# A decoder layer on one core: the shared expert's first 1024 tokens by seven half-size products, with their sums made in earlier stages

## The chip, the core and the metric

The kernel runs on one core of a Trainium2 chip. The metric is device time in microseconds for one execution. TensorE (PE) multiplies, with weight loads (PEld) beside it; VectorE (DVE), ScalarE (ACT) and GpSimd (POOL) do the elementwise work; SyncE (SP) issues nearly all transfers, one after the other, each holding up the ones behind it while it waits for a tile to come free.

## What is computed

4096 tokens of 512 numbers pass through three residual blocks, all in 32-bit floats: a first attention against fixed keys and values with a squared ReLU, a cross attention to 128 context tokens with 16 heads, and a mixture of experts. Each block works on a layer norm of its input. The block that the change touches is the last, cut to what matters:

```python
x = hidden_states.reshape(-1, h)                       # 4096 x 512, the normalised tokens ("z" in the kernel)
shared_out = _swiglu(x, shared_gate_w, shared_up_w, shared_down_w)   # every token; 512 -> 1024 -> 512
logits = x @ gate_w                                    # 32 experts, the best one per token
topk_ids = jnp.argmax(logits, axis=-1)
topk_val = jnp.max(logits, axis=-1)
xs = x * jax.nn.sigmoid(topk_val)[:, None]
# ... tokens sorted by expert, routed_out = the chosen expert's swiglu of xs ...
return shared_out + routed_out                         # added to the residual
# _swiglu(x, gw, uw, dw) = (silu(x @ gw) * (x @ uw)) @ dw
```

## The kernel before

Every 32-bit factor of a matmul is split into a high part (rounded by ACT, `split`, L94) and a low part (the difference, L97, by DVE or POOL), and each product is three matmuls: low by high, high by low, high by high (`three`). A product costs so the matmuls and, once for each factor, two elementwise operations.

Stages follow each other on the tokens. Instructions are recorded in the order in which Python emits them; a scheduler then sets the order on each engine from priorities (`later` lowers one) and from its own estimate of when inputs are ready. Background work is given as generators, and `next(...)` at chosen places sets how far it goes.

- **Stage 0** (`stage0`, about 0 to 785 us): the first attention, 8 tiles of 512 tokens, 4 heads, 16 key blocks each. A score step is three matmuls into a bank of P1 or P2, a ReLU on ACT (L349), the square on DVE (L353), a split, and, seven steps later, three value matmuls (L309). Its background is `context_steps`: keys, values and weights of the cross attention. From the second tile on one background step is taken at `kt % 8 == 6` in every head but the first.
- **Stage 1** (`stage1`, to about 1440 us): the cross attention, 16 tiles of 256 tokens, four groups `q4` of four heads each: `queries`, `scores`, `turn`, `values`, `outputs` at distances of up to five groups. `finish(t)` adds the residual (`xr`, written to `x2`), normalises, transposes (`tr`), splits and stores z (`zT`), stores the unsplit z (`zF`, for tiles past the third), and makes the router's logits (`lt`, `lg`). Its background, near the end, is `shared_weights`.
- **Shared expert** (`shared`, about 1387 to 1830 us): hidden columns 0 to 767, in three pairs of 128-column blocks; the last 256 columns are spread over the routed stage. For tokens 1024 to 4095, three groups G of 1024, each pair p takes Strassen-Winograd's form: a 2 x 2 block product by seven half-size products (`PRODUCTS`, in the order `TURN`), with sums of z (S1 to S4) and of weights (T1 to T4). For the first 1024 tokens the product is plain: `plain_up` (L926, banks P3 and P2) and `plain_down` (L940), in two halves of 512 tokens.
- **Routed experts** (`routed`, to the end).

`Pairs.sums(p)` loads the four weight blocks of a pair (`in_sgu`), forms the four sums (L853), splits them and stores both parts in DRAM (`wS`); `Pairs.steps(p, w)` gives the seven weight tiles of a pair, four split from the raw blocks and three read back from `wS`. Before, `sums(0)` and `sums(1)` run beside the plain products and `sums(2)` in the first step of G = 1. `sums(g, zF, G, ...)` loads z from `zF` and makes S1 to S4, which `load_z` then splits.

In a (G, p) step, `up` makes 7 products x 2 (gate, up) x 2 x 3 matmuls of 512 columns (L975), `down` of the step before follows in `between`; `acc` gathers the pairs and the residual.

Large tiles come from few pools: A to K in one, `raw` (6 tiles) for what is loaded and then split, `W` (45 tiles) for weights, and PSUM banks P1 to P4, two of each.

Of the kernel before, what the change touches and what calls it, by code (L numbers as in the profile page):

```python
# [22 lines left out]
C = 512  # L23
# [15 lines left out]
PAIRS = 3  # L39
# [130 lines left out]
def context_steps(g, ctxT, wk, wv, wq, wo, kst, vst):  # L170
# [28 lines left out]
    for c in range(2):  # L199
        v = yield from weight_steps(g, wv[:, c * 512:(c + 1) * 512], 4, 512, "wv", pool)  # L200
        for b in range(2):
# [12 lines left out]
            yield  # L214
    g.wq2 = yield from weight_steps(g, wq, 4, 1024, "wq", pool)
# [4 lines left out]
def stage0(g, x, wfcT, wpT, lnT, x1, background):  # L220
# [107 lines left out]
    for i, (t, h, kt) in enumerate(steps):  # L328
# [6 lines left out]
        if t > 0 and h > 0 and kt % 8 == 6:  # L335
            with g.after(*marks):
                next(background, None)
# [34 lines left out]
def stage1(g, x1, mask, kst, vst, gate, x2, zT, zF, xs, ef, background):  # L372
# [146 lines left out]
    def finish(t):  # L519
# [3 lines left out]
        for s in range(2):  # L523
            v = g.tile("G", "xr")
            nc.sync.dma_start(v[:], x1[rows[s], :])
            z.append(v)
# [62 lines left out]
    for _ in range(2):  # L589
        go(pre, 1, prep)  # L590
    queries(0, 0)
    queries(0, 1)
    for i in range(4 * NT + 12):
# [22 lines left out]
        for _ in range({4 * NT - 2: 5, 4 * NT + 2: 3}.get(i, 0)):  # L616
            next(background)
# [163 lines left out]
def shared_weights(g, wg, wu, wd):  # L781

    g.sw = {}
    for name, w in (("g", wg), ("u", wu)):
        g.sw[name] = o = [[], []]
        for k in range(4):
            if k % 2 == 0:
                pair = [g.piece("sw", (128, 2, 256)) for _ in range(2)]
            for z in range(2):
                o[z].append([g.piece("sw")[:], pair[z][:, k % 2, :]])  # L790
            yield from split_steps(g, w[k * 128:k * 128 + 128, 0:768], o[0][k:], o[1][k:])
    g.sw["d"] = yield from weight_steps(g, wd[0:768, :], 6, 512, "sd")

# [107 lines left out]
def load_z(g, zT, SUM, G, name, engine):  # L901

    z = z_tiles(g, name)
    for j in range(2):
        if name[0] == "S":
# [8 lines left out]
def shared(g, zT, zF, x2, out, pairs, wd, routing, rest, rest_weights):  # L914
    nc = g.nc
    NG = T // 1024
    Z, H, ACC, SUM = {}, {}, {}, {}

    def plain_up(t, c, z):
        o = []  # L920
        for nm, tag in (("g", "P3"), ("u", "P2")):
            p = g.bank(tag, nm)
            n = 0
            for k in range(4):
                for w, y in three((g.sw[nm], z)):
                    nc.tensor.matmul(p[:], part(w, k, c), y[k][:], start=n == 0, stop=n == 11)  # L926
                    n += 1
            o.append(p)
        s = g.tile("H", "s")
        nc.scalar.activation(s[:], o[0][:], AF.Silu)  # L930
        nc.vector.tensor_tensor(o[1][:], o[1][:], s[:], A.mult)
        hh, hl = g.tile("C", "hh", FR), g.tile("D", "hl", FR)
        split(g, hh[:], hl[:], o[1][:])
        H[t, c] = (hh, hl)

    def plain_down(t, s):
        o = g.bank("P1" if t == 0 and s > 1 else "P4", "d")
        for c in range(2 * PAIRS):
            for n, (w, y) in enumerate(three((g.sw["d"], H[t, c]))):
                nc.tensor.matmul(o[:], y[:, s * 128:(s + 1) * 128], w[c][0], start=c == 0 and n == 0, stop=c == 2 * PAIRS - 1 and n == 2)  # L940
        b = g.tile("I", "b")
        nc.sync.dma_start(b[:], x2[rows(0, t, s), :])
        nc.vector.tensor_tensor(b[:], o[:], b[:], A.add)
        nc.sync.dma_start(out[rows(0, t, s), :], b[:])
# [72 lines left out]
    w = {}  # L1017
    parts = sums(g, zF, 1, SUM, nc.vector)
    ahead = chain(pairs.sums(0), pairs.sums(1), pairs.steps(0, w))
    for t in range(2):  # L1020
        z = [[g.tile(("EF", "AB")[t][i], f"z{i}", FR) for _ in range(4)] for i in range(2)]
        for k in range(4):
            for i in range(2):
                nc.sync.dma_start(f32(z[i][k][:]), zT[i, :, k, t * 512:(t + 1) * 512])
        for c in range(2 * PAIRS):
            if c == 1 and t > 0:
                for s in range(4):
                    plain_down(0, s)
            plain_up(t, c, z)
            if t == 1 or c > 1:  # L1030
                next(ahead, None)
                if t == 1 and c < 3:
                    next(ahead, None)
            if t == 1:
                next(parts, None)
    for n in TURN:
        a = PRODUCTS[n][1]
        Z[a] = load_z(g, zT, SUM, 1, a, nc.vector)
        next(ahead, None)
    run(ahead)  # L1040
    pairs.engine = nc.gpsimd
    steps = [(G, p) for G in range(1, NG) for p in range(PAIRS)]
    before, parts = [lambda s=s: plain_down(1, s) for s in range(4)], None
    for n, (G, p) in enumerate(steps):
# [6 lines left out]
        more = pairs.sums(2) if n == 0 else None  # L1051

        def between(a):
# [5 lines left out]
            if p == PAIRS - 1 and G + 1 < NG:  # L1059
                Z[a] = load_z(g, zT, SUM, G + 1, a, nc.gpsimd)  # L1060
            if before:
                before.pop(0)()
            if more:
                next(more, None)
# [495 lines left out]
```

## Time and profile before

| | us |
|---|---|
| median of 3 runs | 2699.37 (2699.36 to 2700.18) |
| the profiled execution | 2698.85 |
| its span, first to last instruction | 2697.1 |
| PE busy | 2639.6 |
| DVE busy | 2033.8 |
| ACT busy | 1873.8 |
| POOL busy | 1129.3 |

The profile is of one execution. Its windows give each engine's busy time in a stretch of the span and, after an "x", how many instructions touch it; PEclk is the share of full clock that TensorE was granted. Matmuls overlap: the duration of one is longer than the distance between two starts. A row of instructions reads: line, engine, operation, output from inputs, count, shortest, median and longest duration in ns.

### The profile page before, as it was taken

What the parts mean: (1) busy time and instruction counts of PE and PEld (TensorE: products, weight loads), DVE (VectorE), ACT (ScalarE), POOL (GpSimd) and SP (SyncE); (2) the same over time, 40 slices, a digit from 0 to 9 for tenths busy, and PEclk for the clock granted to TensorE, in tenths of its full rate; (3) what the DMA queues carried; (4) which work ended last, traced back from release to release, by engine and by line L of the source; (5) the groups of instructions that cost most, each with busy time, mean ns of one, the idle gap of its engine ahead of it and who ended that gap; (6) DMA issues with size and microseconds to landing.
All of it is one profiled execution on the core that took longest, in us unless ns stands there. A gap on an engine that the chain in (4) does not pass through costs nothing. (4 is left out here: it accounts for less than half of the span.)

```text
span 2697.1 us, 47526 instructions
## 1 busy us (share of the span) xinstructions
PE 2639.6 (98%) x14629; PEld 2274.4 (84%) x14629; DVE 2033.8 (75%) x4559; ACT 1873.8 (69%) x4152; POOL 1129.3 (42%) x911
## 2 busy tenths in 40 slices
PE   7999999999999999999999999999999999999998
PEld 5878888887879999999987878778889898888886
DVE  7777777777777888888876596564776777778995
ACT  7788787888778877877874333333666777767885
POOL 5576566666654334444440547620122122212321
PEclk9999999999999999999999999999999999999999
DMA  4112112212020224232249846673899899999994
GB/s 154 32 63 87 55 67 81 77 43 83 30 86 27 87 76 138 96 108 90 102 158 327 273 140 239 223 214 109 260 287 276 279 302 292 299 280 291 325 324 142
DMA packets 269409, 446.68 MB, mean 166 GB/s; under 512 B 33536, under 2 KB 77568, under 8 KB 269152
## 3 DMA queue, kind: packets, MB, share of 16 engines
q1 hardware_dynamic: 254464, 416.46, 45.6%
q0 software_dynamic: 14688, 27.17, 5.1%
q8 instruction: 116, 1.90, 0.3%
q14 instruction: 141, 1.16, 0.1%
HBM read 348.83 MB, written 96.64 MB: 165 GB/s over the span
## 5 line engine op out<-in xcount | busy, mean ns | idle before, releaser
L97 DVE TENSOR_TENSOR rl<-raw,rh 128x512 fp32r<-128x512 f32 x768 | 488.2, 683 | 90.6 <-ACT rh L94 64.0
L94 ACT CAST rh<-raw 128x512 fp32r<-128x512 f32 x768 | 438.3, 621 | 141.6 <-DMA raw<-in_rg 98.2
L97 POOL TENSOR_TENSOR pl<-p,ph 128x512 fp32r<-128x512 f32 x320 | 411.4, 1297 | 264.3 <-ACT ph L94 210.0
L349 ACT ACTIVATE rl<-s 128x512 f32<-128x512 f32 x512 | 293.2, 604 | 38.2 <-PE s L345 30.6
L1336 POOL DMA_INDIRECT out_dram<-v,idx x46 | 114.2, 2483 | 463.6 <-ACT v L1334 368.7
L470 POOL TENSOR_TENSOR e<-e,ri 128x512 f32<-128x512 f32 x128 | 132.8, 1043 | 305.8 <-DVE ri L468 159.4
L353 DVE TENSOR_TENSOR p<-s,rl 128x512 f32<-128x512 f32 x320 | 215.1, 683 | 41.7 <-ACT rl L349 39.1
L94 ACT CAST ph<-p 128x512 fp32r<-128x512 f32 x320 | 199.2, 626 | 60.1 <-DVE p L353 57.4
L467 ACT ACTIVATE e<-e,mn 128x128 f32<-128x128 f32 x512 | 199.9, 392 | 27.9 <-DVE mn L462 26.7
L345 PE MATMUL s<-qh,kwl 128*128 128x512 f32 x512 | 205.5, 403 | 6.4 <-DVE p L353 3.1
L309 PE MATMUL o<-pl,vwh 128*128 128x512 f32 x512 | 203.1, 397 | 2.2 <-POOL pl L97 2.2
L353 DVE TENSOR_TENSOR s<-s,rl 128x512 f32<-128x512 f32 x192 | 133.3, 694 | 91.2 <-ACT rl L349 90.8
L309 PE MATMUL o<-ph,vwl 128*128 128x512 f32 x512 | 200.9, 394 | 1.0 <-ACT ph L94 1.0
L345 PE MATMUL s<-ql,kwh 128*128 128x512 f32 x512 | 200.3, 391 | 0.0
L345 PE MATMUL s<-qh,kwh 128*128 128x512 f32 x512 | 200.1, 391 | 0.0
L309 PE MATMUL o<-ph,vwh 128*128 128x512 f32 x512 | 199.6, 390 | 0.0
L975 PE MATMUL gu<-z,swh 128*128 128x512 f32 x504 | 158.3, 392 | 0.0
L440 PE MATMUL q<-yh,wql 128*128 128x256 f32 x512 | 147.3, 288 | 1.5 <-ACT yh L94 0.6
L97 DVE TENSOR_TENSOR pl<-s,ph 128x512 fp32r<-128x512 f32 x192 | 131.1, 683 | 21.1 <-ACT ph L94 18.6
L440 PE MATMUL q<-yh,wqh 128*128 128x256 f32 x512 | 146.3, 286 | 0.0
L440 PE MATMUL q<-yl,wqh 128*128 128x256 f32 x512 | 145.9, 285 | 0.0
L345 PEld LDWEIGHTS s<-qh,kwl 128*128 128x128 f32 x512 | 96.6, 189 | 33.1 <-DVE p L353 8.6
(361 smaller groups left out, 7958.0 us busy)
## 6 DMA issues: line engine op xcount, KB each, us to landing
raw<-in_rg SPq DMA_DIRECT2D x256, 256.0 KB, 5.4
raw<-in_ru SPq DMA_DIRECT2D x256, 256.0 KB, 5.4
raw<-in_rd SPq DMA_DIRECT2D x256, 256.0 KB, 5.3
z<-zT SPq DMA_DIRECT2D x116, 256.0 KB, 5.6
b<-x SPq DMA_DIRECT2D x40, 256.0 KB, 3.0
raw<-in_sgu SPq DMA_DIRECT2D x39, 256.0 KB, 4.2
swh<-wS SPq DMA_DIRECT2D x36, 256.0 KB, 4.9
swl<-wS SPq DMA_DIRECT2D x36, 256.0 KB, 4.9
```

The lines of the kernel that those rows point to most:

```text
L94: g.nc.scalar.copy(hi, src)
L97: g.low = (lo_engine or g.nc.vector).tensor_tensor(lo, src, f32(hi), A.subtract)
L309: nc.tensor.matmul(o[:], w, y[:], start=kt == 0 and n == 0, stop=kt == 15 and n == 2)
L345: nc.tensor.matmul(s[:], w, y[:], start=n == 0, stop=n == 2)
L349: m0 = nc.scalar.activation(r[:], s[:], AF.Relu)
L353: m1 = nc.vector.tensor_tensor(p[:], s[:], r[:], A.mult)
L440: nc.tensor.matmul(o[:, i, :], part(w, k, p), y[k // 2][:, k % 2, :], start=n == 0, stop=n == 11)
L467: nc.scalar.activation(e[:, hs], e[:, hs], AF.Exp, bias=mn[:, h:h + 1], scale=-1.0, accum_out=su[:, h:h + 1])
L470: nc.gpsimd.tensor_tensor(e4, e4, ri[:].unsqueeze(2).to_broadcast([128, 4, 128]), A.mult)
L975: nc.tensor.matmul(o[:], y, z, start=(at, x) not in begun, stop=j == 1 and m == 2, skip_group_check=True)
L1336: nc.gpsimd.indirect_dma_start(out=out, out_offset=bass.IndirectOffsetOnAxis(ap=idx[rows, b + j:b + j + 1], axis=0), in_=v[rows], in_offse ...
```

## The change

The first 1024 tokens become the group G = 0 of the same seven-product path, so the plain path and its weights (`shared_weights`) go, and the steps are twelve instead of nine.

- `Pairs.sums(0)` to `sums(2)` move into stage 0, into `context_steps`, two sums to a step, with the low parts on DVE. To make room, background steps are also taken in the heads 2 and 3 of the first tile.
- `zF` is stored for all tiles. `first_sums`, called once in every second group from group 28 to group 59 of stage 1, forms S1 to S4 of the first 1024 tokens from it, splits them and stores them in a new DRAM tensor `zS`.
- `first_steps` replaces `shared_weights` as stage 1's background: weight tiles and inputs of the first step (G = 0, p = 0), of which S inputs are read from `zS`.
- The residual tile `xr` of the last two tiles of stage 1 comes from `raw` rather than G; `up` takes its banks in the order P3, P2, P1 rather than P1, P2, P3.
- Routing (`route`) advances from the third step of twelve rather than from the first of nine.

```diff
 # context_steps, between the values' weights and wq
+    for p in range(PAIRS):
+        steps = g.pairs.sums(p)
+        for _ in steps:
+            next(steps)
             yield
 ...
 # stage0
-        if t > 0 and h > 0 and kt % 8 == 6:
+        if (h > 0 if t > 0 else h > 1) and kt % 8 == 6:
             with g.after(*marks):
                 next(background, None)
 ...
+def first_sums(g, zF, zS):
+
+    V = g.nc.vector
+    for j in range(2):
+        for q in range(2):
+            cols = slice(q * 256, q * 256 + 256)
+            a = []
+            for half, tag in enumerate("rC"):
+                shape = [128, 2, 256]
+                v = g.raw.tile(shape, F32, name="sa", tag="raw") if tag == "r" else g.tile(tag, "sb", F32, shape)
+                at = half * 512 + q * 256
+                g.nc.sync.dma_start(v[:], zF[:, :, at:at + 256].rearrange("p (c j) n -> p j c n", j=2)[:, j, :, :])
+                a.append(v)
+            yield
+            (p, r), s = a, g.W.tile([128, 2, 256], F32, name="sc", tag="W")
+            V.tensor_tensor(s[:, 0, :], r[:, 0, :], r[:, 1, :], A.add)
+            V.tensor_tensor(r[:, 0, :], p[:, 0, :], r[:, 0, :], A.subtract)
+            V.tensor_tensor(s[:, 1, :], s[:, 0, :], p[:, 0, :], A.subtract)
+            V.tensor_tensor(r[:, 1, :], p[:, 1, :], s[:, 1, :], A.subtract)
+            yield
+            for n, v in ((0, s), (2, r)):
+                hi, lo = g.tile("C", "sh", FR, (128, 2, 256)), g.tile("D", "sl", FR, (128, 2, 256))
+                split(g, hi[:], lo[:], v[:])
+                for i, x in enumerate((hi, lo)):
+                    g.nc.sync.dma_start(zS[i, n:n + 2, :, j, cols].rearrange("n p c -> p n c"), f32(x[:]))
+                yield
 ...
 # finish
-            v = g.tile("G", "xr")
+            v = g.tile("G", "xr") if t < NT - 2 else g.raw.tile([128, 512], F32, name="xr", tag="raw")
 ...
-            for c in range(2 if t > 3 else 0):
+            for c in range(2):
                 v = g.tile("D", "zf", F32, (128, 2, 256))
 ...
 # stage1's loop over groups
-        for _ in range({4 * NT - 2: 5, 4 * NT + 2: 3}.get(i, 0)):
-            next(background)
+        if 28 <= i < 60 and i % 2:
+            next(early, None)
+        if i > 4 * NT - 3:
+            next(background, None)
+        if i in (4 * NT - 2, 4 * NT - 1, 4 * NT):
+            next(background, None)
 ...
 # load_z
+        if name[0] == "S" and G == 0:
+            for i in range(2):
+                g.nc.sync.dma_start(f32(z[j][i][:]), zS[i, int(name[1]) - 1, :, j, :])
+            continue
 ...
+def first_steps(g, zT, zS, w, Z):
+
+    ahead = g.pairs.steps(0, w)
+    for n in TURN:
+        a = PRODUCTS[n][1]
+        if a in ("A11", "S2", "S1"):
+            Z[a] = load_z(g, zT, zS, None, 0, a, None)
+        next(ahead)
+        yield
+    for n in TURN:
+        a = PRODUCTS[n][1]
+        if a not in Z:
+            Z[a] = load_z(g, zT, zS, None, 0, a, None)
+            yield
 ...
 # up
-        banks = [[g.bank(tag, "gu") for _ in range(2)] for tag in ("P1", "P2", "P3")]
+        banks = [[g.bank(tag, "gu") for _ in range(2)] for tag in ("P3", "P2", "P1")]
 ...
 # shared: plain_up, plain_down, shared_weights and the loop over the two plain halves go
-    ahead = chain(pairs.sums(0), pairs.sums(1), pairs.steps(0, w))
 ...
-    steps = [(G, p) for G in range(1, NG) for p in range(PAIRS)]
-    before, parts = [lambda s=s: plain_down(1, s) for s in range(4)], None
+    steps = [(G, p) for G in range(NG) for p in range(PAIRS)]
+    before, parts = [], None
 ...
-        more = pairs.sums(2) if n == 0 else None
 ...
-            next(routing, None)
+            if n > 1:
+                next(routing, None)
```

More of the change, by code (lines that the diff above doesn't have):

```diff
@@ L369, in place, with stage1 @@
     return slice(at * 256, at * 256 + 256)
-def stage1(g, x1, mask, kst, vst, gate, x2, zT, zF, xs, ef, background):
+def first_sums(g, zF, zS):
[23 more added lines that the diff above has]
+                yield
+def stage1(g, x1, mask, kst, vst, gate, x2, zT, zF, zS, xs, ef, background):
     nc = g.nc
@@ L590, in stage1 @@
         go(pre, 1, prep)
+    early = first_sums(g, zF, zS)
     queries(0, 0)
@@ L777, in route @@
     nc.sync.dma_start(ids[:], parts[0][:])
[L781 to L792, printed above, removed]
 PRODUCTS = {1: (0, "A11", "B11"), 2: (0, "A12", "B21"), 3: (2, "S4", "B22"), 4: (1, "A22", "T4"),
@@ L898, in z_tiles, with load_z @@
     return [[g.tile(next(tags), "z", FR) for _ in range(2)] for _ in range(2)]
-def load_z(g, zT, SUM, G, name, engine):
+def load_z(g, zT, zS, SUM, G, name, engine):
     z = z_tiles(g, name)
     for j in range(2):
+        if name[0] == "S" and G == 0:
+            for i in range(2):
+                g.nc.sync.dma_start(f32(z[j][i][:]), zS[i, int(name[1]) - 1, :, j, :])
+            continue
         if name[0] == "S":
@@ L911, in load_z, with shared @@
     return z
-def shared(g, zT, zF, x2, out, pairs, wd, routing, rest, rest_weights):
+def first_steps(g, zT, zS, w, Z):
[10 more added lines that the diff above has]
+            Z[a] = load_z(g, zT, zS, None, 0, a, None)
+            yield
+def shared(g, zT, zF, x2, out, pairs, wd, w, Z, routing, rest, rest_weights):
     nc = g.nc
     NG = T // 1024
[L917 to L944, printed above, removed]
+    H, ACC, SUM = {}, {}, {}
     def rows(G, half, s):
@@ L1015, in down @@
             nc.sync.dma_start(out[r, :], b[:])
-    w = {}
-    parts = sums(g, zF, 1, SUM, nc.vector)
-    ahead = chain(pairs.sums(0), pairs.sums(1), pairs.steps(0, w))
[L1020 to L1040, printed above, removed]
     pairs.engine = nc.gpsimd
-    steps = [(G, p) for G in range(1, NG) for p in range(PAIRS)]
-    before, parts = [lambda s=s: plain_down(1, s) for s in range(4)], None
+    steps = [(G, p) for G in range(NG) for p in range(PAIRS)]
+    before, parts = [], None
     for n, (G, p) in enumerate(steps):
@@ L1059, in between @@
             if p == PAIRS - 1 and G + 1 < NG:
-                Z[a] = load_z(g, zT, SUM, G + 1, a, nc.gpsimd)
+                Z[a] = load_z(g, zT, None, SUM, G + 1, a, nc.gpsimd)
             if before:
                 before.pop(0)()
-            if more:
-                next(more, None)
-            next(routing, None)
+            if n > 1:
+                next(routing, None)
         up(G, p, w, between)
@@ L1493, in build @@
         zF = d.tile([128, 4, T], F32, name="zF")
+        zS = d.tile([2, 4, 128, 2, 512], F32, name="zS")
         wS = d.tile([PAIRS, 4, 2, 128, 512], F32, name="wS")
@@ L1510, in build @@
                     nc.sync.dma_start(v[:], empty[:])
+            g.pairs = Pairs(g, I["sgu"], wS)
             stage0(g, I["x"], I["wfcT"], I["wpT"], I["lnT"], x1,
@@ L1515, in build @@
             nc.sync.dma_start(xs[T:T + 1, :].rearrange("o (p k) -> (o p) k", p=128), zero[:])
-            stage1(g, x1, I["mask"], kst, vst, I["gate"], x2, zT, zF, xs, ef, shared_weights(g, I["sg"], I["su"], I["sd"]))
+            w, Z = {}, {}
+            stage1(g, x1, I["mask"], kst, vst, I["gate"], x2, zT, zF, zS, xs, ef, first_steps(g, zT, zS, w, Z))
             rest = Rest(g, zT, out)
-            shared(g, zT, zF, x2, out, Pairs(g, I["sgu"], wS), I["sd"],
+            shared(g, zT, zF, x2, out, g.pairs, I["sd"], w, Z,
                    route(g, ef, I["tab"], I["tri"], lists, ids, plan, idx), rest, rest_weights(g, I["sg"], I["su"], I["sd"]))
```

## The prediction

> **What bounds the kernel now.** I read the page first. TensorE is busy 98% of the span, in every slice but the first and the last; so what counts is how many matmuls there are, at what pace they start, and where TensorE is short of work.
>
> ```profile
> PE 2639.6 (98%) x14629; PEld 2274.4 (84%) x14629; DVE 2033.8 (75%) x4559; ACT 1873.8 (69%) x4152; POOL 1129.3 (42%) x911
> ```
>
> Then the windows, ten microseconds each, where the second attention hands over to the shared expert (columns: engine's busy time and instructions, granted clock, DMA share, GB/s).
>
> ```profile
> 1390.00:1400.00 10.00, 9.40 (x49) 7.11 (x48) 9.91 (x21) 6.46 (x13) 1.28 (x1) 1.00 0.38 126
> ...
> 1420.00:1430.00 10.00, 9.06 (x39) 6.58 (x38) 5.10 (x14) 4.36 (x8) 0.00 (x0) 1.00 1.07 394
> 1430.00:1440.00 10.00, 5.19 (x14) 3.79 (x13) 6.82 (x22) 6.72 (x11) 0.71 (x1) 0.66 0.61 228
> 1440.00:1450.00 10.00, 9.06 (x47) 7.20 (x47) 8.16 (x12) 4.34 (x8) 3.33 (x2) 1.00 0.76 243
> ...
> 1460.00:1470.00 10.00, 10.00 (x46) 8.29 (x45) 9.08 (x16) 5.15 (x11) 0.00 (x0) 1.00 1.05 392
> ```
>
> The last row is full speed: 46 matmuls touch a window, two of them cut by its edges, so 44 starts in 10 us, 0.227 us each. The reader is to see the hole above it: 7.3 us idle (0.60 + 0.94 + 4.81 + 0.94), and around 1435 a clock of 0.66. The waits and the timeline name it:
>
> ```profile
> PE g L926 <- ACT s L930: 4.8, 1, 4.8
> 1435.30 5.17 PE L926 MATMUL g<-z,sw 128*128 128x512 f32 x12 [4.81 <-ACT s L930]
> SPq L942 <- PE av L497: 7.7, 1, 7.7
> ```
>
> Twelve matmuls took 5.17 us instead of 11 x 0.227 + 0.39 = 2.9: the slow clock cost 2.3 us more. SyncE stood 7.7 us at the residual load `b<-x` of the old path, and the weight loads queued behind it came late. So the hand-over loses about 9.6 us.
>
> Last, rows that price what the change moves, and how full the engines are where it goes (stage 0, then stage 1):
>
> ```profile
> 400.00:600.00 200.00, 200.00 (x911) 164.59 (x910) 153.09 (x279) 162.47 (x325) 130.02 (x106) 1.00 0.21 69
> 1060.00:1360.00 300.00, 299.23 (x2167) 278.96 (x2166) 246.16 (x978) 237.34 (x753) 131.76 (x122) 1.00 0.30 100
> L853 DVE TENSOR_TENSOR raw<-raw x8: 675/688/1782, 1443.0 to 1462.8; 128x512 f32<-128x512 f32 x8
> L97 DVE TENSOR_TENSOR z<-zs,z x8: 678/1441/1778, 1471.0 to 1508.7; 128x512 fp32r<-128x512 f32 x8
> L97 DVE TENSOR_TENSOR pl<-s,ph x192: 652/681/693, 23.1 to 781.7; 128x512 fp32r<-128x512 f32 x192
> ```
>
> **The change, part by part.**
>
> *Products.* The plain path makes 2 halves x 6 column blocks x 24 = 288 up and gate matmuls of 512 columns for the first 1024 tokens. Seven products of 12 matmuls for three pairs are 252. The down products stay 144 (48 x 3 before, 3 x 8 x 6 after). 36 fewer on the path. The row of these matmuls says 389 ns each, which would make 14.0 us; but they overlap, and the windows show a start every 0.227 us. The Trainium skill ("TensorE: Matmul & The Clock Gate", the part on back-to-back matmuls) has N / 2.4 GHz + 2.5 ns between starts, 215.7 ns at 512 columns, so 7.8 us; I take the measured pace: 36 x 0.227 = **-8.2 us**. Weight loads (188 ns) fit under a matmul.
>
> *Hand-over.* Out go 16 loads and splits of gate and up weights, 6 splits of down weights, 16 plain inputs, the residual loads `b` with SyncE's 7.7 us stand, and four of seven ACT table loads (1.28 us each). In come seven weight pairs (four split on chip, three read ready-made from `wS`), 28 transfers of z, two loads of `sd`. Before the first pair is through, that is 28 + 4 + 6 = 38 transfers of 256 KB, 10 MB, about what the old path fetched there. With the windows' 390 GB/s one takes 0.65 us, so 25 us; the loads begin near 1374 and the last products (inputs in A and B tiles, free only after the last attention values) are wanted near 1430. In the built order 24 products stand inside the attention's tail (66 before), 44 after its last output product, while layer norm and transposes of the last tile run; that chain took 1424.7 to 1440 before, and 44 x 0.227 = 10 us cover most of it. Two of the new products want the P1 banks that the last tile's output sums leave. Bounds: all 9.6 us of loss gone, or a loss as large plus 25 - 19 = 6 us in which transfers outlast the pair's 84 products. I take 3.6 us of loss left: **-6 us**.
>
> *Sums of weights, now in stage 0.* Twelve loads, 12 ACT casts (0.62 us), 12 differences and 12 low parts on DVE, 24 writes to `wS`. Context steps start earlier to make room (four in the first tile), so `wq` and `wo` end two slots later, with stage 1 still 20 us away. By the row, 24 x 0.69 = 16.5 us of DVE and 7.4 of ACT; SyncE issues 36 x 0.4 us and only the next tile's loads queue behind. TensorE covers it as long as DVE keeps up. But the six steps come one in eight score steps, 12.3 us; there DVE already has 0.765 x 12.3 = 9.4 us, and 4 x 0.69 make 12.2: just full. Here a rule speaks against the change: by the Trainium skill ("SBUF — State Buffer", the two separate sides) a DVE operation with two SBUF inputs and a GpSimd operation reading SBUF exclude each other for their whole length. The rows agree: a DVE operation with one input in PSUM never exceeds 0.693 us, though POOL is 65% busy there, while `raw<-raw` reaches 1.78 and `z<-zs,z` has a median of 1.44. All 24 new operations have two SBUF inputs. At 65% POOL time I estimate 0.69 + 0.65 x 0.75 = 1.18 us, so a step of eight has 14.1 us of DVE in 12.3: 1.8 us too much, 11 us over six. Score tiles rotate through four banks and the value products trail by seven steps, so DVE can run behind, and it catches up afterwards. Nearest evidence of what is felt: at 600 to 650 us DVE had 40.7 of 50 and TensorE lost 2.1. Bounds: nothing (0.69, no lag), 11 us (all of it). I take **+2.5 us**. Without the bank cover it would be the 11.
>
> *Sums of inputs, in stage 1.* Eight more POOL additions `zf` (1.29 us; POOL is 44% busy), 16 DVE additions of 256 columns (about 0.37, estimated as half the 0.69 row plus its fixed part), 8 splits (ACT 0.62, DVE 0.69), 32 transfers against a DMA share of 0.30. DVE gets 11.5 us over 300, to 86% from 82%, with collisions to 88%. At 88% (1200 to 1250 us) TensorE was idle 0.15 us. The transfers pass SyncE's queue between the attention's own loads, and the `sa` and `sb` loads wait only for tiles long free; the `zS` writes wait for splits, and behind them stand the next tile's `xt` loads, a whole tile early. Bounds 0 and 6 us (all of the 2% collisions); **+1.5 us**.
>
> *Steps of G.* The nine (G, p) steps lose 2.14 + 0.91 + 3.08 + 0.82 = 7 us to waits for DVE and `acc` at 1500 to 1750, most at a change of G and under the routing tables. Twelve steps with one change more, whose sums and splits (8 x 1.3 us + 8 x 1.3) move from DVE to POOL, add a third to a half: **+3 us**. Routing starts at the third step, near 1490 instead of 1507; its cover stays. Bounds 0 and 6.
>
> *Sum:* -8.2 - 6 + 2.5 + 1.5 + 3 = -7.2. The profiled execution took 2698.85 us (span 2697.1), so 2691.65; the median of the runs lies 0.5 us above it: 2692.2.
>
> **The rivals.** 0.2%, about what a measurement of this kernel can tell from no change, is 5.4 us: 2694.0 and 2704.8.
>
> (a) *The hand-over is bound by its transfers.* For: DMA share 1.07 at 1420, 10 MB for 19 us of products, in-order SyncE. Against: half of the inputs' tiles are free before the tail. Then the 9.6 us stay: -8.2 + 0 + 7 = -1.2, 2698; with 4 us more, 2702. No change.
>
> (b) *DVE becomes the bound in stage 0.* One mechanism, at about 490 to 590 us: every one of the 24 operations meets POOL. At 1.78 us a step of eight has 9.4 + 7.1 = 16.5 us for 12.3: 4.2 too much, 25 over six, less about 5 us of lag that banks allow, +20. Sum: -8.2 - 6 + 20 + 4.5 = +10, 2709.7. It ends slower by over 0.2% from where stage 0 costs 15.1 us: 20.1 / 6 = 3.35 too much per step, a mean of (12.3 + 3.35 - 9.4) / 4 = 1.56 us. Against: POOL idles a third of the time, and loses 2.6 us of low parts per step there.
>
> (c) *Everything is covered.* -8.2 - 9.6 + 2 = -15.8, 2683.5. For: TensorE has 100% in 400 to 600 now. Against: two-input collisions are in the rows.
>
> That the products do not fall is excluded by their count.
>
> **How the numbers follow.** Forecast (2686 to 2694): 0.48. (c): 0.10. (a), with costs that cancel the gain: 0.31. (b): 0.11. The likeliest is 2692.2. The range leaves out most of (b) and the far part of (c): 2685.5 to 2702. Faster 0.58, same 0.31, slower 0.11.
>
> **What would show it.** In the profile after: 672 + 336 `gu` matmuls, a page with some 36 fewer on TensorE; at 1390 to 1450 idle under 4 us and no clock under 0.9; `raw<-raw` on DVE at 490 to 590 with a mean near 1.2 us, TensorE idle there under 3 us. The forecast is wrong if that mean passes 1.5 and TensorE waits for `p` or `rl` (rival b), or if TensorE waits at `gu` for z or `swh` transfers by over 8 us (rival a).

## The result, and the profile after

The changed kernel took 2723.11 us (median of 5 runs, 2721.97 to 2724.83) against 2699.46 (2699.36 to 2704.04) for the one before, run beside it: a ratio of 1.0089, interval 1.0078 to 1.0101. It is slower by 23.7 us. The forecast was 2692.2, in a range to 2702.

The profiled execution of it has a span of 2721.2 us, 24.1 more than before. First the page's line of engines.

```profile
PE 2646.0 (97%) x14593; PEld 2268.1 (83%) x14593; DVE 2087.1 (77%) x4593; ACT 1872.5 (69%) x4155; POOL 1189.5 (44%) x948
```

TensorE has 36 matmuls less, as counted, and yet 6.4 us more of busy time; VectorE has 53.3 us more. The extra operations are all there, and they are not free. The windows say where it was felt (engine's busy time and instructions, clock, DMA share, GB/s): stage 0 in the first two rows, stage 1 in the third.

```profile
400.00:600.00 200.00, 193.62 (x862) 153.54 (x860) 171.04 (x281) 158.39 (x307) 121.97 (x94) 1.00 0.28 100
500.00:600.00 100.00, 94.79 (x417) 72.95 (x415) 95.44 (x143) 78.63 (x148) 59.55 (x45) 1.00 0.41 146
1060.00:1360.00 300.00, 290.49 (x2063) 267.00 (x2061) 257.15 (x970) 232.41 (x733) 129.31 (x117) 0.99 0.34 116
```

Compare with the rows of before, which the prediction shows. TensorE had all 200 us of the first window, and 911 matmuls touched it; now 862. Not all of these 49 are lost pace: 24 are products of the context (`cv`), which the early places put ahead of 400 us. Of score and value products alone 766 start there in place of 797, so 31 x 0.227 = 7 us are lost. In the third window the kinds of products are nearly in the same proportion, and 2063 stand for 2167. Busy time falls there by only 3%, the count by 4.8%: matmuls overlap, so a gap shorter than an overlap leaves no idle time, and time at a lower clock counts as busy. Between windows with the same kinds of products the count is the better reading of a lost pace.

The hand-over, which the forecast wanted repaired, is repaired.

```profile
1420.00:1430.00 10.00, 9.44 (x51) 7.59 (x50) 4.98 (x11) 7.26 (x18) 4.61 (x4) 1.00 0.99 371
1430.00:1440.00 10.00, 9.28 (x53) 7.26 (x53) 9.77 (x28) 6.68 (x14) 1.96 (x2) 1.00 0.71 222
1440.00:1450.00 10.00, 9.79 (x46) 7.43 (x47) 5.53 (x16) 3.29 (x7) 5.04 (x4) 1.00 1.03 361
1450.00:1460.00 10.00, 10.00 (x46) 8.27 (x45) 7.33 (x20) 4.14 (x6) 2.00 (x2) 1.00 1.05 395
```

The 4.8 us hole and the clock of 0.66 are gone. TensorE's waits of 1380 to 1470 us sum to 7.1 us before and 1.9 after, with none added up to 1520 us (the hand-over lies 26 us later now). The wait of the chain of before, for `s` on ACT, has no successor there.

The new waits stand elsewhere. These are TensorE's (what waits, for whom: us in all, times, longest), at 480 to 620, at 1150 to 1400 and at 1690 to 1710 us; "..." parts the three.

```profile
PE s L350 <- DVE p L358: 3.5, 5, 1.0
PE o L314 <- POOL pl L97: 0.6, 2, 0.3
...
PE pt L516 <- DVE yl L97: 7.3, 3, 2.4
PE av L530 <- DVE ql L97: 2.3, 6, 0.5
...
PE gu L991 <- DVE u L998: 6.1, 1, 6.1
```

All but one of them wait for VectorE, in all three stages.

Some of these waits cost more than their length. Two of the three waits for `yl` are followed by 3.4 us at half of the granted clock (here the one that ends at 1196.7), the third is not. In the wait for `u` the clock fell as well, and it stayed at half for 4 us after it:

```profile
1198.00:1201.40 3.40, 3.40 (x18) 3.40 (x17) 3.10 (x20) 2.18 (x10) 1.28 (x1) 0.50 0.01 3
1201.40:1205.00 3.60, 3.60 (x26) 3.23 (x25) 1.45 (x3) 2.83 (x11) 1.04 (x1) 1.00 0.00 0
...
1706.00:1710.00 4.00, 4.00 (x9) 2.96 (x10) 3.96 (x5) 1.95 (x4) 4.00 (x4) 0.50 0.28 78
```

There the query matmuls start every 0.214 us in place of 0.118, the `gu` matmuls every 0.427 us in place of 0.227. So such a stretch costs an estimated 1.7 to 2 us more, half of its length.

### The profile page after: what moved, and what is told of

It is laid out like the page before. It is cut to its first block, busy times and chain, and to the rows that moved or that the text cites. A ratio compares the mean times of both kernels' runs of the same rounds, so it can differ in the third digit from the quotient of the medians.

```text
span 2721.2 us, 47660 instructions
## 1 busy us (share of the span) xinstructions
PE 2646.0 (97%) x14593; PEld 2268.1 (83%) x14593; DVE 2087.1 (77%) x4593; ACT 1872.5 (69%) x4155; POOL 1189.5 (44%) x948
## 5 line engine op out<-in xcount | busy, mean ns | idle before, releaser
L991 PE MATMUL gu<-z,swh 128*128 128x512 f32 x672 | 209.8, 391 | 0.6 <-DMA z<-zT 0.6
L991 PEld LDWEIGHTS gu<-z,swh 128*128 128x128 f32 x672 | 126.6, 189 | 27.0 <-DMA z<-zT 1.0
L991 PE MATMUL gu<-z,swl 128*128 128x512 f32 x336 | 131.8, 396 | 12.5 <-DVE u L998 6.1
```

What stands on the lines that cost most here:

```text
L991: nc.tensor.matmul(o[:], y, z, start=(at, x) not in begun, stop=j == 1 and m == 2, skip_group_check=True)
```

## The experiments

To compare many kernels, four points of each profile are enough: the start of the first query matmul of stage 1 (the end of stage 0), of the last output matmul of stage 1, of the last down product of the shared expert, and the span. Stage 0 is the first point, stage 1 the distance from it to the second, the shared steps from there to the third. What follows the third takes 878 to 882 us in every kernel. The points are those of one profiled execution each. The changed kernel and eight others have the same code in stage 0; their first points lie from 799.5 to 803.4, so a difference of less than 4 us in one mark decides nothing by itself.

| kernel | stage 0 | stage 1 | shared | ratio to before (95%) |
|---|---|---|---|---|
| before | 786.3 | 638.2 | 390.9 | 1 |
| after | 799.6 | 651.1 | 390.4 | 1.0089 (1.0078 to 1.0101) |
| e1_no_weight_sums | 793.5 | 648.0 | 389.3 | 1.0067 (1.0051 to 1.0084) |
| e5_weight_sums_on_pool | 796.2 | 649.2 | 389.4 | 1.0060 (1.0043 to 1.0076) |
| e6_old_slots | 791.0 | 651.1 | 392.7 | 1.0055 (1.0038 to 1.0071) |
| e11_old_slots_no_sums | 787.4 | 649.5 | 391.2 | 1.0029 (1.0018 to 1.0040) |
| e2_no_first_sums | 800.1 | 632.2 | 390.8 | 1.0026 (1.0015 to 1.0038) |
| e3_first_sums_on_pool | 801.4 | 632.4 | 387.9 | 1.0032 (1.0019 to 1.0044) |
| e7_only_additions_on_dve | 803.4 | 637.9 | 388.4 | 1.0042 (1.0027 to 1.0058) |
| e8_only_low_parts_on_dve | 801.8 | 633.9 | 389.5 | 1.0031 (1.0019 to 1.0044) |
| e4_routing_a_step_later | 800.3 | 650.4 | 381.8 | 1.0064 (1.0048 to 1.0081) |
| e9_splits_off_pool | 799.5 | 650.5 | 385.8 | 1.0087 (1.0072 to 1.0102) |
| e10_splits_off_pool_ninth | 800.9 | 649.7 | 385.5 | 1.0081 (1.0065 to 1.0098) |
| b1_pool_and_routing | 800.7 | 632.4 | 381.6 | 1.0002 (0.9993 to 1.0011) |
| b2_fewer_sums_early | 791.0 | 632.3 | 389.3 | 0.9994 (0.9987 to 1.0001) |
| b3_sums_off_dve_old_slots | 782.4 | 635.5 | 383.3 | 0.9945 (0.9932 to 0.9959) |

Before and after are not to be subtracted blindly in the two middle columns: before, 66 products of the shared expert stand ahead of the last output matmul, after it 24 (30 in e3, e7 and the three kernels b; counted in the traces). So 42 x 0.227 = 9.5 us of work has moved from "stage 1" to "shared", and for the same work stage 1 is 22.4 us longer than before, not 12.9.

### Stage 0: the sums, or the places of the steps

The theory was that the sums of weights fill VectorE; the rival, that the background steps taken in the first tile disturb the score steps, with or without the sums.

**Without the sums of weights** (e1_no_weight_sums; the weight tiles T1 to T4 are loaded from the stored z instead, so the products with them are other products):

```diff
-    for p in range(PAIRS):
-        steps = g.pairs.sums(p)
-        for _ in steps:
-            next(steps)
-            yield
 ...
-                    self.g.nc.sync.dma_start(f32(w[b][i][:]), self.wS[p, int(b[1]) - 1, i])
+                    self.g.nc.sync.dma_start(f32(w[b][i][:]), self.g.zT[i, :, int(b[1]) - 1, 512 * p:512 * p + 512])
```

> The changed kernel without the sums of weights in stage 0; the three weight inputs T of each step are read from stored z of the same size instead, so that part of the output is not computed. Context steps stay where the change put them. Theory A (the 24 added DVE operations with two SBUF inputs fill DVE in stage 0 and TensorE waits): the first query matmul of stage 1 comes at 786 to 790 us, as before the change (786.3), instead of 799.6; total about 2712 (2709 to 2715) against 2723.1. Theory B (the earlier context steps and the re-sorted order cost, not the operations): first query at 796 or later, total 2719 or more.

Stage 0 ended at 793.5, between the two theories. So 6.1 of the 13.3 us went with the sums (their loads, casts and stores included), and 7.2 stayed: the early places became a suspect of equal size.

**The sums on POOL** (e5_weight_sums_on_pool): differences and low parts by POOL, where stage 0 leaves it 35% of the time.

```diff
+    g.pairs.engine = pool
     for p in range(PAIRS):
 ...
+    g.pairs.engine = nc.vector
```

> The changed kernel with the sums of weights of stage 0 (12 differences, 12 low parts) on POOL instead of DVE, nothing else. Without those sums the first query matmul came at 793.5 us instead of 799.6. Theory A (DVE was full at 500 to 600 us): first query near 794, total 6 us less than the changed kernel, about 2717 on the earlier scale (ratio to before near 1.0065). Rival (any engine that takes them delays the square or the low part that TensorE waits for): first query at 799 or later, ratio 1.009 or more.

796.2, 3.4 of the 6.1 us back. One mark does not tell 3.4 us; the ratios do, 1.0060 against 1.0089, whose intervals do not meet. Its window at 500 to 600:

```profile
500.00:600.00 100.00, 97.03 (x441) 78.53 (x440) 76.58 (x129) 81.33 (x157) 82.22 (x67) 1.00 0.41 140
```

VectorE is back from 95.4 to 76.6, POOL up to 82.2, and TensorE has 97.0 in place of 94.8. Half a result: part of stage 0's loss was the load on VectorE, and most of the rest has another cause.

**The old places** (e6_old_slots): the sums stay on VectorE, the first tile takes no background steps.

```diff
-        if (h > 0 if t > 0 else h > 1) and kt % 8 == 6:
+        if t > 0 and h > 0 and kt % 8 == 6:
```

> The changed kernel with stage 0's background taken in the old places only (no steps in the first tile), so the 43 steps have 42 places and the six sums lie later, in the sixth tile and the seventh. Theory B (the other 7 us of stage 0, which stayed without the sums, come from the context steps being earlier): first query near 793, ratio near 1.006. Rival D (they come from where the casts of wq and wo, or the sums, meet the next tile's layer norm, wherever they start): first query still at 798 to 802, ratio 1.008 to 1.010.

791.0: the early places cost 8.6 us with the sums in.

**Old places and no sums** (e11_old_slots_no_sums; both edits, and e1's other products with it) is the fourth corner.

> The changed kernel without the sums of weights in stage 0 (the three T inputs of each step are read from stored z instead, so that part is not computed) and with the background in the old places. With the early places and no sums the first query matmul came at 793.5 us; with the old places and the sums at 791.0; before the change at 786.3. If the early places alone cost the rest, it comes at 785 to 788 here. If something else of stage 0 costs (the writes of zF or the pool's order), it stays at 791 or later.

787.4, within 1.1 of before. Now the square is full: the early places cost 6.1 us without sums (787.4 to 793.5) and 8.6 with; the sums 3.6 us in the old places and 6.1 in the early ones. The difference of 2.5 between them is within the scatter of the marks, and the 3.6 is too (the intervals of e6 and e11 overlap slightly). The two causes are of like size, and together they make 12.2 of the 13.3 us.

How the places act is seen beside the sums' stretch. These are 300 to 400 and 400 to 500 us of e1, then of e11, neither of which has a sum of weights:

```profile
300.00:400.00 100.00, 98.91 (x446) 80.58 (x445) 74.28 (x133) 79.27 (x156) 61.84 (x50) 1.00 0.19 64
400.00:500.00 100.00, 98.82 (x447) 80.66 (x446) 75.57 (x139) 80.48 (x161) 61.53 (x50) 1.00 0.19 64
...
300.00:400.00 100.00, 99.63 (x471) 81.97 (x470) 77.34 (x139) 81.65 (x160) 60.71 (x49) 1.00 0.20 69
400.00:500.00 100.00, 100.00 (x456) 82.35 (x455) 75.62 (x138) 80.92 (x162) 63.77 (x52) 1.00 0.20 66
```

The counts of the first pair of rows differ mostly by kind: e11 has 36 short products of the context there, e1 has 24 long ones. Score and value products alone are 391 in e1 against 398, then 389 against 398: about 2 us lost in each 100. No other engine is more than about 1 us busier in e1, and TensorE waits little: at 380 to 490 three times, 0.5 us for `ph`, 0.3 and 0.2 us for `pl`, where e11 does not wait at all.

What differs is the built order. In e11 score and value products alternate through all of stage 0 exactly as before the change; in e1 they do so differently from the first tile on. So the places cost not by work but, as it seems, by the order that the scheduler made of it. Why it sorts so, and which detail of the order costs, was not tried.

### Stage 1: what the sums of inputs cost

Theories: the transfers and casts; the additions on VectorE, colliding with POOL; or the low parts, which put more in front of the attention's own chain.

**Without them** (e2_no_first_sums; the S inputs of G = 0 are read from the stored z, so they are not sums), and **all of them on POOL** (e3_first_sums_on_pool):

```diff
-        if 28 <= i < 60 and i % 2:
-            next(early, None)
 ...
-                g.nc.sync.dma_start(f32(z[j][i][:]), zS[i, int(name[1]) - 1, :, j, :])
+                g.nc.sync.dma_start(f32(z[j][i][:]), zT[i, :, (int(name[1]) - 1) % 2 * 2 + j, 0:512])
```

> The changed kernel without first_sums in stage 1; the S inputs of the first 1024 tokens are read from zT instead of zS, so those sums are not computed. Theory A (the added DVE work with two SBUF inputs delays the tiles in which it lies): the three stalls near 1194, 1278 and 1361 us and the smaller ones beside them go, stage 1 becomes some 12 us shorter, total about 2711 (2708 to 2714). Theory B (the order of yl and the layer norm's chain on DVE is what the schedule of stage 1 now is, whatever the sums do): the stalls stay, total 2718 or more.

```diff
-    V = g.nc.vector
+    V = g.nc.gpsimd
 ...
-                split(g, hi[:], lo[:], v[:])
+                split(g, hi[:], lo[:], v[:], V)
```

> The changed kernel with first_sums' additions and low parts on POOL instead of DVE; same transfers, same ACT casts, same result. Theory A (DVE's share is what costs): like the run without first_sums, 2711 to 2715. Rival C (what costs is the ACT casts, tiles held or transfers, or POOL's own use of SBUF against DVE): 2718 or more.

Stage 1 took 632.2 and 632.4 us, against 651.1. On VectorE the sums of inputs cost 18.7 us; on POOL nothing that these marks show. The transfers and ACT's casts are the same in e3, so they cost nothing that shows either. Some 3.5 of the 22.4 us stay when the sums are left out (e2), and no run tells their cause. The window of e3 at 1060 to 1360:

```profile
1060.00:1360.00 300.00, 299.39 (x2167) 278.90 (x2166) 250.02 (x989) 243.66 (x764) 152.19 (x146) 1.00 0.37 123
```

2167 matmuls touch it, exactly as many as before the change.

**Which part of them.** e7_only_additions_on_dve puts only the low parts on POOL, e8_only_low_parts_on_dve only the additions.

```diff
 # e7
-                split(g, hi[:], lo[:], v[:])
+                split(g, hi[:], lo[:], v[:], g.nc.gpsimd)
 # e8
-    V = g.nc.vector
+    V = g.nc.gpsimd
 ...
-                split(g, hi[:], lo[:], v[:])
+                split(g, hi[:], lo[:], v[:], g.nc.vector)
```

> The changed kernel with first_sums' 16 additions on DVE as in the change, and the 8 low parts on POOL. All on POOL stage 1 took 632.4 us from the first query matmul to the last output matmul, all on DVE 651.1. Theory A1 (the loss follows the DVE time added, 15 us of additions and 8 us of low parts): 641 to 646. Theory A2 (it is the burst of four additions, which make ql and the following chain late): 648 to 652. Theory A3 (it is the low parts): 632 to 637.

> The complement of the run with only the additions on DVE: first_sums' additions on POOL, its 8 low parts on DVE. Stage 1, from the first query matmul to the last output matmul, took 632.4 us with both on POOL, 637.9 with the additions on DVE, 651.1 with both on DVE. If the costs add, the low parts alone cost 13 us: 644 to 647. If the 13 us need both (the low parts alone lie elsewhere in time, at 1207 and 1228 us, than the stalls near 1171, 1182 and 1194), the stage takes 632 to 638, and the order into which the two together push the next tile's yl is the cause.

637.9 for e7, outside every window that was set for it, and 633.9 for e8. The additions alone cost 5.5 us, the low parts alone 1.5 (less than the marks scatter), both 18.7: far more than their sum. TensorE's longest items at 1150 to 1400 are, in e7 and then in e8:

```profile
PE q L473 <- DVE v L533: 3.1, 6, 0.9
...
PE tr L417 <- DVE pl L97: 0.5, 1, 0.5
```

Neither has the item `pt <- yl` of 7.3 us. That belongs to both together. It lies in three groups of waits of 3.4 us each (0.5, 0.2, 0.2 and 2.4), two tiles apart, which end at 1196.7, 1280.9 and 1363.6 us. With the two stretches of half clock behind them they make 10.3 + 3.4 = 13.7 of the 18.7 us. Here is one, with what goes before it (start, duration, engine, instruction; in brackets the idle time before it and its releaser):

```profile
1276.10 1.04 POOL L503 TENSOR_TENSOR e<-e,ri 128x512 f32<-128x512 f32 x1 [3.07 <-DVE bv L138]
1277.11 0.70 POOL L139 TENSOR_TENSOR bp<-bv,mhalf 128x2 f32<-128x2 f32 x1
1277.84 0.99 DVE L140 SCALAR_TENSOR_TENSOR bt<-bp,bv 128x2 f32<-128x2 f32 x1 [1.00 <-POOL bp L139]
...
1280.17 0.68 DVE L97 TENSOR_TENSOR yl<-tr,yh 128x512 fp32r<-128x512 f32 x1
1280.91 0.66 PE L516 MATMUL pt<-ident,e 128*128 128x128 f32 x4 [2.45 <-DVE yl L97]
```

VectorE, which works in its built order, stands a whole microsecond waiting for `bp`, a small step of a layer norm that POOL runs behind `e`. The second `yl` is queued behind the five steps that follow `bp` (two of `bt`, one of `br`, two of `xr`), and TensorE, at `pt`, waits for that `yl`. So an engine can be idle, and its idleness be the delay of another.

In the built order of VectorE the two `yl` of such a tile stand seven places apart in the kernel after, five before the change and in e3 and e7. That the costs of e7 and e8 do not add is shown. That the order is what multiplies them was not tried alone, and distance by itself does not do it: in e8 two pairs of `yl` stand ten places and 4.6 us apart, and TensorE does not wait for them.

The additions, priced at 0.37 us each, are here in the kernel after and, last line, in e7:

```profile
L392 DVE TENSOR_TENSOR sc<-sb x4: 1118/1125/1416, 1083.0 to 1330.2; 128x256 f32<-128x256 f32 x4
L393 DVE TENSOR_TENSOR sb<-sa,sb x4: 909/913/915, 1084.9 to 1331.9; 128x256 f32<-128x256 f32 x4
L395 DVE TENSOR_TENSOR sb<-sa,sc x4: 403/823/826, 1087.8 to 1334.8; 128x256 f32<-128x256 f32 x4
...
L395 DVE TENSOR_TENSOR sb<-sa,sc x4: 402/402/406, 1090.8 to 1329.1; 128x256 f32<-128x256 f32 x4
```

0.40 is the undisturbed price; the 16 of the kernel after took 0.97 on average. What lengthens them runs on POOL at the same moment (POOL's line first, then VectorE's):

```profile
1249.80 2.90 POOL L578 TENSOR_TENSOR zf<-zh,zl 128x512 f32<-128x512 f32 x2
...
1250.64 0.90 DVE L394 TENSOR_TENSOR sc<-sc,sa 128x256 f32<-128x256 f32 x1
1252.16 0.82 DVE L395 TENSOR_TENSOR sb<-sa,sc 128x256 f32<-128x256 f32 x1
```

The first addition ends 0.28 us after the first of POOL's two operations, the second 0.28 us after the second: each waits for the one that runs, and then goes. VectorE's operations with one input in PSUM between them took their usual 0.68. POOL's two took 1.47 and 1.49 where they take 1.29 alone.

### The steps of G: the routing list's minimum

TensorE's waits at 1470 to 1760 sum to 7.0 us before, 13.6 after; 6.1 of these are one stall. VectorE and POOL at that moment:

```profile
1698.36 6.97 DVE L813 TENSOR_TENSOR list<-list 128x110 int32<-128x110 int32 x2 [5.28 <-DMA list<-list]
1705.24 0.69 DVE L998 TENSOR_TENSOR u<-gu,p 128x512 f32<-128x512 f32 x1
...
1697.75 0.96 POOL L803 DMA_INDIRECT list<-small  x1 [0.30 <-issue]
1698.73 2.50 POOL L97 TENSOR_TENSOR z<-zs,z 128x512 fp32r<-128x512 f32 x2
1701.19 1.25 POOL L97 TENSOR_TENSOR swl<-raw,swh 128x512 fp32r<-128x512 f32 x1
1702.41 2.47 POOL L97 TENSOR_TENSOR z<-zs,z 128x512 fp32r<-128x512 f32 x2
```

Two minima of the routing lists, 110 elements wide, took 6.97 us together, 6.66 of them the first; `u`, for which TensorE waits, comes directly after. The first minimum began while POOL still issued an indirect transfer of the lists, and POOL's five operations followed that without a pause. The rows of the three minima are, in the kernel after, before the change, and in the two that follow:

```profile
L813 DVE TENSOR_TENSOR list<-list x3: 274/1306/6657, 1698.4 to 1705.8; 128x110 int32<-128x110 int32 x3
...
L775 DVE TENSOR_TENSOR list<-list x3: 275/275/936, 1709.8 to 1716.4; 128x110 int32<-128x110 int32 x3
...
L813 DVE TENSOR_TENSOR list<-list x3: 264/807/997, 1736.6 to 1739.3; 128x110 int32<-128x110 int32 x3
...
L813 DVE TENSOR_TENSOR list<-list x3: 261/275/2990, 1697.0 to 1702.5; 128x110 int32<-128x110 int32 x3
```

**Routing one step later** (e4_routing_a_step_later) takes the minimum out of the change of G, when POOL splits a new group's inputs:

```diff
-            if n > 1:
+            if n > 2:
```

> The changed kernel with routing begun at the fourth step of twelve instead of the third. The profile shows one DVE operation of the routing (the minimum of two lists) taking 6.66 us at 1698 us while POOL runs five operations back to back, and TensorE waits 6.1 us. Theory A (the minimum meets the splits of a change of G on POOL, by its place): the 6.1 us go, total 2717 (2715 to 2719). Rival (TensorE would have waited there for the split of a weight anyway, or routing now ends too late for the routed experts): 2722 to 2728.

The third row above: the longest minimum took 0.997 us, TensorE's waits fell to 8.1 us, and the shared steps from 390.4 to 381.8. That is 8.6 us for 5.5 of waits; the 4 us at half clock behind the stall are gone too. The total, 2714.95, is at the lower end of theory A's range.

**The splits off POOL** (e9_splits_off_pool, then e10_splits_off_pool_ninth) leave routing where it is and give the splits of one step's inputs to VectorE.

```diff
-                Z[a] = load_z(g, zT, None, SUM, G + 1, a, nc.gpsimd)
+                Z[a] = load_z(g, zT, None, SUM, G + 1, a, nc.vector if n == 8 else nc.gpsimd)
```

> The changed kernel with the splits of S inputs for G = 2 (made in the sixth step) on DVE instead of POOL; routing stays in its place. There one minimum of two lists took 6.66 us on DVE. Theory A (a DVE operation with two SBUF inputs is held off as long as POOL runs operations on SBUF back to back): with POOL free the three minima take about 0.3 us each and the 6 us stall of TensorE goes, total 4 to 7 us less (ratio near 1.0065). Rival (the minimum's time is that of its transfers or of its descriptor, not of POOL): one minimum stays over 4 us, ratio 1.008 or more.

> The changed kernel with the splits of S inputs for G = 3 (made in the ninth step, where the minima of the lists fall) on DVE instead of POOL. Theory A (a DVE operation with two SBUF inputs is held off while POOL runs back to back): no minimum over 2 us, the 6.1 us stall goes, total 4 to 8 us less than the changed kernel, ratio 1.0055 to 1.0075. Rival (DVE waits in order for the lists' transfers, and TensorE for DVE): a stall of 4 us or more stays behind the minima, ratio 1.008 or more.

e9 has `n == 5`, the sixth step, and the minima fall in the ninth, so it did not touch POOL's run beside them. The order shifted nevertheless: its minima took 2.0, 2.9 and 0.26 us, and another stall of 5.6 us (for `acc`) took the place of the old one. Its time says nothing of the theory. e10 hits the step (fourth row above): the longest minimum took 2.99 us, where theory A had set 2 as its limit, and the stall at `u` 2.4 in place of 6.1, where the rival had set 4. POOL's run there was one pair only, again behind an indirect transfer:

```profile
1697.34 2.50 POOL L97 TENSOR_TENSOR swl<-raw,swh 128x512 fp32r<-128x512 f32 x2
1696.99 3.30 DVE L813 TENSOR_TENSOR list<-list 128x110 int32<-128x110 int32 x2 [4.71 <-DMA list<-list]
```

In both kernels the held minimum ends 0.14 us after POOL's last operation of the run: 1698.36 + 6.66 against 1702.41 + 2.47, and 1696.99 + 2.99 against 1697.34 + 2.50. The same holds for every minimum that ran into POOL's work in any of the traces, e9's two among them: each ends 0.13 to 0.14 us after an operation of POOL. With two operations in place of five it is held less than half as long. That decides against the rival, the transfers of the lists. The ratio, 1.0081, does not tell the gain from none; the stall does, and e4 shows what it is worth.

So the minimum lost its turn several times in a row, and the additions of stage 1 did not. Of 528 other VectorE operations with two SBUF inputs in all traces (the additions of 256 columns, the sums and low parts of 512), 522 saw one operation of POOL end before they could run, or none, and six saw two. What sets the minimum apart, its integers, its size or its place in the queue, was not tried.

### What the findings make together

**POOL for the inputs' sums, and routing later** (b1_pool_and_routing: the edits of e3 and e4).

> Both cures together: first_sums on POOL, routing a step later. If the two costs are separate, their gains add: 18 + 8 us off the changed kernel, which is level with the kernel before (ratio 0.998 to 1.002). If both draw on the same slack (POOL's, or the schedule's), the ratio stays at 1.002 or more.

1.0002: the two gains add, 18.7 in stage 1 and 8.8 in the shared steps. It is as fast as before the change, and no faster, since stage 0 still has its loss (800.7).

**Fewer sums in stage 0** (b2_fewer_sums_early): b1, with the old places, and `sums(2)` left in the first step of G = 0.

```diff
-    for p in range(PAIRS):
+    for p in range(PAIRS - 1):
 ...
+        more = pairs.sums(2) if n == 0 else None
 ...
+            if more:
+                next(more, None)
```

> As the last one, and in stage 0 only the sums of pairs 0 and 1, in the old places; those of pair 2 are made on POOL beside the first step of G = 0. If stage 0's 13 us are the sums' DVE work and the moved context steps, most of it comes back: first query at 790 to 796, ratio 0.995 to 0.998. If it is neither, the ratio equals the last one's.

0.9994, no difference that can be told. Against b1, stage 0 gained 9.7 us and the shared steps gave back 7.7. TensorE's waits at 1380 to 1470 sum to 6.4 us (1.9 in the kernel after), most of them for a ready-made weight on its way and for a low part on POOL:

```profile
PE gu L991 <- DMA swl<-wS: 4.0, 2, 3.2
PE d L1023 <- POOL dwl L97: 1.3, 1, 1.3
```

So something like rival (a) of the prediction, a hand-over that waits for its transfers, appears when that step carries one more pair's loads and writes. Whether it is the amount, SyncE's order or POOL's splits ahead of them was not tried, and these waits are 4.5 of the 7.7 us. The expected ratio of 0.995 to 0.998 did not come, though stage 0 did as expected.

**All sums off VectorE, old places, routing later** (b3_sums_off_dve_old_slots: the edits of e3, e4, e5 and e6).

> All cures together: first_sums on POOL, routing a step later, stage 0's background in the old places, and the six sums of weights on POOL. Against the run with the first two cures (first query at 800.7 us, ratio 1.0002) the old places are worth 7 to 9 us and POOL instead of DVE 2 to 3: first query near 789, ratio 0.9955 to 0.997, a clear gain over the kernel before. If POOL, now with the sums and the low parts of five score steps in eight, becomes the late one in stage 0, first query at 792 or later and ratio 0.998 or more.

2682.49 us (2678.42 to 2685.31) against 2697.14 beside it: 0.9945, interval 0.9932 to 0.9959. It beats both kernels, as was expected. Its page and its window of 400 to 600:

```profile
PE 2627.9 (98%) x14592; PEld 2268.3 (85%) x14593; DVE 2026.7 (76%) x4545; ACT 1869.3 (70%) x4155; POOL 1222.7 (46%) x996
400.00:600.00 200.00, 199.97 (x909) 164.03 (x908) 152.73 (x278) 162.02 (x325) 140.86 (x114) 1.00 0.25 83
```

TensorE again has all of the window, with the 12 sums in it; POOL went from 130.0 before the change to 140.9 of 200 us. VectorE is 60 us below the changed kernel. Its stage 0, 782.4, is even 3.9 us shorter than before the change and 5.0 shorter than e11's, which has no sums at all. The first is no more than the marks scatter, the second little more. Its order of score and value products differs from that of before from the fifth tile on; whether that is worth anything was not tried.

## Why the prediction was wrong

The prediction failed at what it let VectorE's idle time cover: in stage 0 8.5 of 11 us of overrun, in stage 1 all of the added work but 1.5 us. Beside that it gave the earlier context steps no price. The runs showed a cost of 13.3 us in stage 0 and 18.7 in stage 1. The gains that it forecast came.

**Products.** Right: 672 + 336 `gu` matmuls, 36 fewer. At 0.227 us apiece that is -8.2.

**Hand-over.** Right. -6 was taken; waits fell by 5.2 us and the 2.3 us of slow clock are gone too, -7.5 together. TensorE's idle time at 1390 to 1450 is 2.3 us, under the 4 that were set, and the clock is 1.00 throughout.

**Sums of weights: +2.5 taken, 13.3 measured.** Two terms were mis-sized.

```profile
L97 DVE TENSOR_TENSOR swl<-raw,swh 128x512 fp32r<-128x512 f32 x12 | 15.0, 1274 | 0.0
L876 DVE TENSOR_TENSOR raw<-raw 128x512 f32<-128x512 f32 x12 | 12.4, 1031 | 0.0
```

These groups of 500 to 600 us show that the estimate of collisions was good: (15.0 + 12.4) / 24 = 1.14 us for one operation where 1.18 had been worked out. The rule named there, of the Trainium skill's "SBUF — State Buffer", agrees in kind: of the 24 added operations with two SBUF inputs 15 were stretched, to as much as 1.78 us, and nine were not and took 0.67 to 0.72; the score steps' operations with an input in PSUM stayed at 0.66 to 0.70.

The arithmetic led to an overrun of 11 us, and then the prediction let four banks and a lag of seven steps swallow 8.5 of it. That is one failed step: 6.1 us were felt (e1), and TensorE's idle time at 490 to 590 was 4.4 us where under 3 had been set. VectorE in a stretch at 95.4% ran late, and the lag did not hide it. The choice leaned on a stretch at 81% of VectorE. The other step is "Context steps start earlier to make room", which was given no price at all, only a due date; it cost 6 to 9 us (e6, e11). What it does to the order of TensorE's instructions was not asked.

**Sums of inputs: +1.5 taken, bounds 0 to 6, 18.7 measured.** The largest miss. The additions took 0.97 us in place of 0.37, yet they alone make 5.5 (e7). The failed step is the inference that 88% of VectorE leaves room, because TensorE was idle only 0.15 us in a stretch that full. In the 1060 to 1360 window VectorE is at 257 of 300 us, 86%, as the working had it, and TensorE still does 104 matmuls less. In stage 1 VectorE, POOL and TensorE hand single small steps to each other, and the lines show that it counts when `v` and `yl` come, not how much time is over. Why additions and low parts together cost more than twice what they cost apart stays open.

**Steps of G: +3 taken, 6.6 by the waits.** More than twice that, and above the bound of 6; most of it is one stall. The prediction counted POOL's sums and splits at a change of G as so much work, not as a run without a pause; five in a row hold a minimum on VectorE for 6.66 us. The routing tables' cover was said to stay; the lists' minimum came to lie under those splits instead.

**The sum by these terms:** -8.2 - 7.5 + 13.3 + 18.7 + 6.6 = 22.9, against 24.1 in the spans. That it comes so near is partly luck: marks that scatter by up to 4 us and sums of waits are added, and the 3.5 us of stage 1 without a cause are not in it.

**The rivals.** (b) had the side, the engine and the mechanism, "DVE becomes the bound", and got 0.11. Its price of 1.78 us for one operation did not come (1.14), and the point from which it was to decide, a mean of 1.56, was not reached; the loss came at a lower price, because less was covered, and mostly from causes that it did not name. Neither of the two signs that were to show the forecast wrong came, and it was wrong. (c), everything covered, has 2683.5; b3 took 2682.5, where nothing that was added lies on VectorE. (a) did not come with this change; b2 shows waits of its kind.

## What to carry to other kernels

An elementwise engine with 15 or 20% of idle time has no 15% to give away if the main engine waits for single results of it: ask what is queued ahead of the next result that is awaited, and in which order the build puts it. Where two engines stretch each other's operations, try the added two-input work on the one of them whose results are awaited less, as e3 and b3 do. When an estimate shows an overrun, what is to absorb it must be shown in a stretch that is as full as the one to come.

## What the runs showed of the hardware

- A VectorE operation of 0.27 us was held for 6.66 us over five GpSimd operations in a row, and ended 0.14 us after the last; with a run of two it took 2.99. The Trainium skill ("SBUF — State Buffer", the two separate sides) says that of a VectorE operation with two SBUF inputs and a GpSimd operation that reads SBUF the one that starts first has the shared ports for its whole length and the other blocks. The traces go further in this one case: the minimum did not get its turn between GpSimd operations that followed each other without a pause, and the rest of an indirect transfer that GpSimd was issuing, 0.34 us, held it off as well. The additions did get theirs, between two such operations (1250.64 to 1251.54).
- After two of three waits of 2.4 us on TensorE the granted clock was 0.50 for 3.4 us, and after the third it was not.
- A 256-column addition takes 0.40 us on VectorE undisturbed, 0.82 to 1.51 beside GpSimd (kernel after and e7), and 0.74 on GpSimd itself. Alone, VectorE is the faster engine for it; in this mix it is not. These are GpSimd's rows in e3:

```profile
L392 POOL TENSOR_TENSOR sc<-sb x4: 733/742/745, 1083.4 to 1317.8; 128x256 f32<-128x256 f32 x4
L395 POOL TENSOR_TENSOR sb<-sa,sc x4: 739/740/741, 1089.4 to 1323.8; 128x256 f32<-128x256 f32 x4
```
